# Turning a layer's softmax maxima in bfloat16, with buffers exchanged between queries, tokens and rows

## The chip, the cores and the metric

The kernel runs on one core of a Trainium2 chip. The metric is the device time of one execution in microseconds; the lower, the better. Before the change it is 1400.39 us (median of three runs, 1397.52 to 1403.52).

## What is computed

One transformer layer on x of shape (2, 2048, 256): layer norm, causal attention with 16 heads of 16, residual; layer norm, a gated feed-forward network whose inputs and weights are rounded to 4-bit floats in blocks of 16 (and scaled back), residual. Cut to what matters here:

```python
q, k = rope(split_heads(x @ Wq.T + bq)), rope(split_heads(x @ Wk.T + bk))
att = einsum('bhqd,bhkd->bhqk', q, k) / sqrt(16)
att = softmax(where(mask, att, -inf), axis=-1)
y = einsum('bhqk,bhkd->bhqd', att, v)
x = x + y @ Wo.T + bo
h = silu(fp4_linear(norm(x), w_gate)) * fp4_linear(norm(x), w_up)
x = x + fp4_linear(h, w_down)
```

## The kernel before, in words

Tokens are worked in chunks of 512 (`CH`; four chunks to a batch, eight in all), heads in four groups of four (`GROUP`). That gives 32 slots, one for each chunk and group. For a slot the kernel goes over the scores twice.

*Maxima* (`max_steps`, L1002). For each tile of 128 queries and each chunk of keys up to the diagonal, TensorE makes scores with queries on the partitions (L1020, two strips of 64 rows side by side, one for each of two heads; masks at L988 are bfloat16 matmuls added on the diagonal), and VectorE reduces them to row maxima (L1044). `split` (L1063 to 1085) puts each maximum into the tile `mslots` as a sum of three float32 numbers: of the first two only the upper 16 bits are kept, the third is what is left. `turn` (L1092) transposes `mslots` on TensorE, four times 128x128 (L1098, tile `ptm`), and ScalarE casts the result to the bfloat16 tile `mT` (L1104).

*Values* (`value_steps`, L1127). Scores are made again, this time with keys on the partitions: a bfloat16 matmul of `mT` with a matrix of -1 subtracts the maximum (L1150), a matmul of keys and queries adds the score (L1158), ScalarE takes the exponential (L1173), and TensorE multiplies with the values (L1206), with a column of ones for the denominator. `divide` transposes that back and divides.

The queries of a slot live in a tile `qT` (two head pairs x 512 tokens of float32, 4 KB on each partition), filled from a DRAM scratch `parts` by four DMAs (L866). A slot's maxima and its values both read it. The keys stay resident in `kT` (L879). Beside this run the side steps: the layer norm of the next chunk (tiles `xin`, read at L676, transposed at L694), its projections and rotary embedding (L763 to 879), the rounding of the weights (tile `wr`, which shares the room `xn` with the rows of the feed-forward network, L600), and the feed-forward network of chunks already attended (`ffn_steps`, L1316: rows `x0`, `x1`, `xn`, then L1430 gate and up, L1523 down, L1535 store). The last chunk's feed-forward network uses rooms that have come free, a `qT` room for each tile of 128 tokens.

The order of the work on each engine is not that of the code. Every step is a task with an engine, a cost and a due time, and names what it reads and writes. `Plan.ordered` (L158) plays the tasks through with those costs and picks, engine by engine, the one that can start first, or the most urgent of those that can start within 0.03 us of it. A task that makes a tile of some kind must find a room of that kind free: the dictionary `ROOM` says how many there are, the same number as the pool's buffers. So a count in `ROOM` or a task's cost changes the written order on all engines; the order is then fixed by dependencies between neighbouring instructions (`in_order`, L435). DMAs are all issued from one queue, SP's, in the planned order. A turn costs `turning(4)`, that is 0.01 + 0.13 x 4, in the plan.

Of the kernel before, what the change touches and what calls it, by code (L numbers as in the profile page):

```python
# [29 lines left out]
F32 = mybir.dt.float32  # L30
F32R = mybir.dt.float32r
BF16 = mybir.dt.bfloat16
# [6 lines left out]
P = 128  # L39
# [11 lines left out]
CH = 512  # L51
TPC = CH // P
# [29 lines left out]

XIN = 3
ROOM = dict(ps=7, av=1, ex=4, qT=5, parts=4)
ROOM.update(mx=2, mparts=1, left=1, mT=2, avs=1, den=2, y=2)
ROOM.update(xnT=1, xin=XIN, high=1, t1=1, t2=1, cs=1, dev=XIN-1)
ROOM.update(x0=1, xT=2, x1=2, xn=2, h=1, hrT=1, step=1, fdev=2, sc16=2, sc44=2)


ANY_TURN = ("ps",)
# [196 lines left out]
def turning(n):  # L289

    return 0.01 + 0.13 * n


def landing(kb):
    return 2.0 + kb / 250
# [3 lines left out]
def layer_kernel(  # L299
# [17 lines left out]
    nc = tc.nc  # L317
    B, T, E = x.shape
# [9 lines left out]


    const = ctx.enter_context(tc.tile_pool(name="const", bufs=1))  # L330
    qry = ctx.enter_context(tc.tile_pool(name="qry", bufs=5))
    spill = ctx.enter_context(
        tc.tile_pool(name="spill", bufs=4, space=bass.MemoryType.DRAM)
    )
# [3 lines left out]
    ffn = ctx.enter_context(tc.tile_pool(name="ffn", bufs=2))  # L338
    ps_s = ctx.enter_context(tc.tile_pool(name="ps_s", bufs=7, space=PSUM))
# [7 lines left out]
    ident = const.tile([P, P], F32, name="ident")  # L347
# [26 lines left out]
    for strip in range(2):  # L374
        rows = slice(strip * STRIP, (strip + 1) * STRIP)
# [11 lines left out]
        less.append(t)  # L387
    minus_half = const.tile([P, 1], F32, name="minus_half")
    nc.gpsimd.memset(minus_half, -0.5)
    mslots = const.tile([P, TPC, GROUP, SLOT], F32, name="mslots")  # L390
    nc.gpsimd.memset(mslots, 0.0)

# [35 lines left out]
    def small(cols, name):  # L428

        return ps_s.tile([P, CH], F32, tag="ps", name=name)[:, :cols]  # L430
# [160 lines left out]
    def load_rounded(w, row, rows, col, cols, put, target):  # L591

        st = {}
        raw = Thing("xn")
        scaled, rounded = fp4(lambda: st["raw"], raw, rows, cols)

        def load(due):
            def run():
                st["raw"] = ffn.tile([P, E], F32, tag="xn", name="wr", bufs=2)[:rows, :cols]
                nc.sync.dma_start(st["raw"], w[row : row + rows, col : col + cols])  # L600

            add(SP, landing(128), run, [], [raw], due)

        def turn(due):
            pm = Thing("ps")

            def run():
                pt = small(KE * P, "ptr").rearrange("p (k o) -> p k o", k=KE)
                for k in range(0, cols, P):
                    n = min(P, cols - k)  # L610
                    nc.tensor.transpose(
                        pt[:n, k // P, :rows], st["raw"][:, k : k + n], ident[:rows, :rows]
                    )
                st["pt"] = pt

            add(PE, turning(2), run, [raw, fixed], [pm], due, late=0.05)
            add(ACT, 0.35, lambda: put(st["pt"]), [pm], [target], due)

        return [(0, load), (3, scaled), (2, rounded), (4, turn)]
# [37 lines left out]
    def norm_steps(b, c):  # L657
# [5 lines left out]
        def load(i, due):  # L663
# [5 lines left out]
            def run():  # L669
                if not early:  # L670
                    st[i]["x"] = pre.tile([P, E], F32, tag="xn", name="xin", bufs=XIN)
                else:
# [329 lines left out]
    def max_steps(b, c, g):  # L1002

        steps = []
        st = {}
        mx, parts = Thing("mx"), Thing("mparts")
        found = []
        max_[b, c, g] = Thing("mT")

        def one(i, kc, d, due):  # L1010
            duo = 2 * (g % 2) + d
            cols = CH if kc < c else (i + 1) * P
            ps, got = (Thing("ps"), Thing("ps")), []

            def run():
                qT = qTs[b, c, g]
                kT = kTs[b, kc, g // 2]
                sc = [ps_s.tile([P, CH], F32, tag="ps", name="sc") for _ in range(2)]
                for h in range(2):
                    nc.tensor.matmul(  # L1020
                        sc[h][:, :cols],
                        lhsT=strips(qT, h, d, slice(i * P, (i + 1) * P)),
                        rhs=strips(kT, h, duo, slice(0, cols)),
                        start=True,
                        stop=(kc < c),
                    )
                if kc == c:
                    for h in range(2):
                        masked(sc, h, cols - P, mask_q)
                got.append(sc)  # L1030

            def reduced(h):
                name = "parts" if c else "mx"
                if name not in st:
                    st[name] = att.tile(
                        [P, TPC, 2, 2, NC] if c else [P, TPC, 2, 2],
                        F32,
                        tag=name,
                        name=name,
                        bufs=1 if c else 2,  # L1040
                    )
                at = st[name][:, i, h, d]
                dst = at[:, kc : kc + 1] if c else at.unsqueeze(1)
                nc.vector.tensor_reduce(dst, got[0][h][:, :cols], AX.X, ALU.max)  # L1044

            add(
                PE,
                0.18 + 0.44e-3 * cols if kc == c else 0.27,
                run,
                [qT_[b, c, g], k_[b, kc, g // 2][g % 2], fixed],  # L1050
                [*ps, m_order],
                due,
                [parts if c else mx],
                "strip",
                FEED_M,
                0.07,
            )
            for h in range(2):
                own = Thing(of=parts if c else mx)
                found.append(own)  # L1060
                add(DVE, on_vector(cols), lambda h=h: reduced(h), [ps[h]], [own], due)

        def split(due):  # L1063
            left = Thing("left")

            def run():
                if c:
                    st["mx"] = att.tile([P, TPC, 2, 2], F32, tag="mx", name="mx")
                    nc.vector.tensor_reduce(
                        st["mx"].rearrange("p i h d -> p (i h d)"),  # L1070
                        st["parts"][:, :, :, :, : c + 1].rearrange(
                            "p i h d k -> p (i h d) k"
                        ),
                        AX.X,
                        ALU.max,
                    )

                mx = st["mx"].rearrange("p i h d -> p i (h d)")
                rest = att.tile([P, TPC, GROUP], F32, tag="left", name="left", bufs=1)
                for n, (src, rest) in enumerate(((mx, rest), (rest, mslots[:, :, :, 2]))):  # L1080
                    part = mslots[:, :, :, n]
                    nc.vector.tensor_scalar(
                        part.bitcast(I32), src.bitcast(I32), UPPER, None, ALU.bitwise_and
                    )
                    nc.vector.tensor_tensor(rest, src, part, ALU.subtract)

            if c:
                add(DVE, 1.04, run, found, [mx, left, slots_of], due - 0.1)
            else:
                add(DVE, 0.79, run, found, [left, slots_of], due - 0.1)  # L1090

        def turn(due):  # L1092
            pm = Thing("ps")

            def run():
                st["pt"] = small(CH, "ptm").rearrange("p (i q) -> p i q", i=TPC)
                for i in range(TPC):
                    nc.tensor.transpose(  # L1098
                        st["pt"][:, i, :], mslots[:, i].rearrange("p s d -> p (s d)"), ident
                    )  # L1100

            def put():
                mT = att.tile([P, CH], BF16, tag="mT", name="mT")
                nc.scalar.copy(mT, st["pt"].rearrange("p i q -> p (i q)"))  # L1104
                maxima[b, c, g] = mT

            add(
                PE,
                turning(TPC),
                run,  # L1110
                [slots_of, fixed],
                [pm],
                due - 0.1,
                [max_[b, c, g]],
                late=0.05,
            )
            add(ACT, on_scalar(CH), put, [pm], [max_[b, c, g]], due - 0.1)

        for i in range(TPC):
            for kc in range(c + 1):  # L1120
                for d in range(2):
                    steps.append(lambda due, i=i, kc=kc, d=d: one(i, kc, d, due))
        return steps, split, turn

    rows, rows_ = {}, {}
# [563 lines left out]
    def transpose_biases(due):  # L1689
# [29 lines left out]
        lambda due, i=i, pair=pair: steps[0].stripped(i, pair, due)  # L1719
# [72 lines left out]
```

## Time and profile before

| | |
|---|---|
| Time, median of 3 runs | 1400.39 us (1397.52 to 1403.52) |
| The profiled execution's own time | 1400.22 us |
| Its span from the first to the last instruction | 1398.2 us |
| Mean granted TensorE clock | 0.976 |
| TensorE busy | 1338.2 us |
| VectorE busy | 1117.2 us |
| ScalarE busy | 759.6 us |
| GpSimd busy | 520.7 us |
| Moved by DMA | 69.22 MB, mean 50 GB/s |

All of these are of one profiled execution but the first row. PE is TensorE's matmuls, PEld its loads of weights, which overlap them; DVE is VectorE, ACT ScalarE, POOL GpSimd, SP the engine whose queue issues the DMAs. A group line names the code line, the engine, the operation, the tiles written and read, the shape and the count, then busy microseconds and mean nanoseconds of one, and last the idle time of the engine just ahead of these instructions with what ended it. A line of the time order has start, length (both in us), engine, line, operation and count. Matmuls are pipelined, so the length of one is more than its share of PE's time.

### The profile page before, as it was taken

To read this page: it belongs to the slowest core of one execution; us is meant where nothing else is said; L and a number is where in the kernel's file an instruction comes from. 1 tells how busy PE (TensorE), PEld (TensorE's weight loads), DVE (VectorE), ACT (ScalarE), POOL (GpSimd) and SP (SyncE) were. 2 spreads that over 40 slices of the span, in tenths; PEclk is the share of its full clock that TensorE was granted. 3 is DMA by queue.
4 is the path that set the end of the run, shared out by engine and by line. 5 is a ranking of instruction groups with operands and counts; after the bars stand their busy time and mean duration, and the time that the engine had idled before them with its cause. 6 is when DMAs were issued, how large, how long until landed. Compare 5 with 4: busy or idle time off the path is not lost. (4 is left out here: it accounts for less than half of the span.)

```text
span 1398.2 us, 27614 instructions
## 1 busy us (share of the span) xinstructions
PE 1338.2 (96%) x10437; PEld 675.2 (48%) x10437; DVE 1117.2 (80%) x2442; ACT 759.6 (54%) x1698; POOL 520.7 (37%) x671
## 2 busy tenths in 40 slices
PE   6898999999999999999999999999999999999986
PEld 3454445544544444444465455455454444444454
DVE  6779989988889988875477978998888988983286
ACT  2533665466556556567743455455655556667711
POOL 4655634434413433224353543242442331320342
PEclk9887999999999999999999999999999999999998
DMA  2443424202111301020422404130120120000000
GB/s 91 116 108 80 90 67 93 54 16 61 35 24 53 65 24 41 16 53 25 95 66 53 125 25 90 50 69 12 54 54 5 53 56 11 9 8 9 5 5 15
DMA packets 46316, 69.22 MB, mean 50 GB/s; under 512 B 6372, under 2 KB 22120, under 8 KB 46184
## 3 DMA queue, kind: packets, MB, share of 16 engines
q1 hardware_dynamic: 45888, 67.20, 20.4%
q8 instruction: 82, 1.34, 0.4%
q14 instruction: 50, 0.41, 0.1%
q10 hardware_dynamic: 296, 0.26, 0.1%
HBM read 47.52 MB, written 19.92 MB: 48 GB/s over the span
## 5 line engine op out<-in xcount | busy, mean ns | idle before, releaser
L1173 ACT ACTIVATE ex<-sx 128x512 f32<-128x512 f32 (+3 forms) x1280 | 594.0, 538 | 358.4 <-PE sx L1158 201.5
L1044 DVE TENSOR_REDUCE parts<-sc 128x1 f32<-128x512 f32 (+3 forms) x1152 | 638.9, 612 | 64.0 <-PE sc L1020 41.2
L1158 PE MATMUL sx<-qT,kT 64*128 64x512 f32 (+3 forms) x1280 | 339.2, 521 | 0.0
L1206 PE MATMUL av<-ex,v 128*32 128x512 f32 (+3 forms) x2560 | 300.6, 540 | 0.2 <-ACT ex L1173 0.2
L1020 PE MATMUL sc<-kT,qT 64*128 64x512 f32 (+3 forms) x1280 | 291.2, 430 | 9.1 <-DVE parts L1044 1.9
L1150 PE MATMUL sx<-mT,less 64*128 64x512 bf16 (+3 forms) x1280 | 249.5, 355 | 4.7 <-DVE mx L1044 2.0
L1020 PEld LDWEIGHTS sc<-kT,qT 64*128 64x128 f32 x1280 | 138.5, 190 | 156.9 <-DVE parts L1044 46.8
L517 POOL TENSOR_SCALAR inv<-inv 128x16 f32<-128x16 f32 (+2 forms) x82 | 18.0, 220 | 509.7 <-DVE inv L513 472.0
L1150 PEld LDWEIGHTS <-less 64*128 64x128 bf16 x1280 | 68.6, 94 | 211.1 <-issue 203.5
L1158 PEld LDWEIGHTS sx<-qT,kT 64*128 64x128 f32 x1280 | 132.6, 195 | 8.9 <-issue 6.5
L1523 PE MATMUL pd<-wdT,hrT 128*128 128x256 f32 (+1 forms) x384 | 103.6, 410 | 0.7 <-ACT hrT L1300 0.3
L1206 PEld LDWEIGHTS av<-ex,v 128*32 128x32 f32 x2560 | 52.0, 108 | 74.2 <-issue 65.9
L1523 PEld LDWEIGHTS pd<-wdT,hrT 128*128 128x128 f32 (+1 forms) x384 | 70.0, 197 | 29.8 <-issue 15.6
L1430 PE MATMUL pg<-wgT,xT 128*128 128x352 f32 x224 | 77.1, 478 | 1.0 <-ACT qb L776 0.3
L1044 DVE TENSOR_REDUCE mx<-sc 128x1 f32<-128x128 f32 (+3 forms) x128 | 54.6, 479 | 25.8 <-PE sc L988 25.6
L1430 PE MATMUL pg<-wuT,xT 128*128 128x352 f32 x224 | 74.3, 472 | 0.2
L763 PE MATMUL pj<-xnT,wqkT 128*128 128x512 f32 x128 | 73.3, 671 | 1.1 <-DVE v L954 0.6
L542 POOL TENSOR_TENSOR h<-h,step 128x704 f32<-128x704 f32 x28 | 47.2, 1686 | 68.6 <-DVE step L539 66.9
L988 PE MATMUL sc<-pick,mask_q 64*128 64x64 bf16 x1024 | 70.9, 201 | 0.0
L1456 ACT ACTIVATE h<-pg 128x352 f32<-128x352 f32 x64 | 30.0, 469 | 69.2 <-PE pg L1430 59.6
L815 POOL TENSOR_TENSOR t<-t,cs 128x512 f32<-128x512 f32 x31 | 39.6, 1279 | 75.1 <-DVE t L809 70.5
L988 PE MATMUL sx<-pick,mask_k 64*128 64x64 bf16 x1024 | 64.1, 196 | 0.0
(153 smaller groups left out, 1592.1 us busy)
## 6 DMA issues: line engine op xcount, KB each, us to landing
qT<-parts SPq DMA_DIRECT2D x120, 128.0 KB
kT<-parts SPq DMA_DIRECT2D x120, 128.0 KB
parts<-high SPq DMA_DIRECT2D x30, 256.0 KB
parts<-t SPq DMA_DIRECT2D x30, 256.0 KB
cs<-in_rope_dram SPq DMA_DIRECT2D x8, 512.0 KB
xin<-in_L_attn_x_dram SPq DMA_DIRECT2D x28, 128.0 KB
x<-in_L_attn_x_dram SPq DMA_DIRECT2D x28, 128.0 KB
out_dram<-x SPq DMA_DIRECT2D x28, 128.0 KB
```

What stands on the lines that cost most here:

```text
L542: queue.tensor_tensor(src(), src(), st["step"], ALU.add)
L763: nc.tensor.matmul(got["pj"], lhsT=wqkT[:, k, i, cols], rhs=xnTs[b, c][:, k, :], start=(k == 0), stop=(k == KE - 1),)
L815: (nc.gpsimd if early and i == 0 else queue).tensor_tensor(swapped, swapped, angles[b, c][:, 1, :], ALU.mult)
L988: nc.tensor.matmul(sc[h][:, col + at : col + at + STRIP], lhsT=strips(mask, h, half), rhs=strips(pick, h), start=False, stop=(half == 1),)
L1020: nc.tensor.matmul(sc[h][:, :cols], lhsT=strips(qT, h, d, slice(i * P, (i + 1) * P)), rhs=strips(kT, h, duo, slice(0, cols)), start=True, ...
L1044: nc.vector.tensor_reduce(dst, got[0][h][:, :cols], AX.X, ALU.max)
L1150: nc.tensor.matmul(sc[h][:, off:], lhsT=strips(less[d], h), rhs=strips(mT, h, slice(off, CH)), start=True, stop=False,)
L1158: nc.tensor.matmul(sc[h][:, off:], lhsT=strips(kT, h, duo, slice(jj, jj + P)), rhs=strips(qT, h, d, slice(off, CH)), start=False, stop=(j ...
L1173: nc.scalar.activation(st[j, d][:, h, off:], got[0][h][:, off:], AF.Exp, scale=HD**-0.5)
L1206: nc.tensor.matmul(st["av"][SLOT * s : SLOT * (s + 1), off:], lhsT=v[:, at : at + SLOT], rhs=st[j, d][:, h, off:], start=(j == 0), stop=(j ...
L1430: nc.tensor.matmul(got[half], lhsT=split("xrT")[:, k, :], rhs=wT[:, k, half * IH : (half + 1) * IH], start=(k == 0), stop=(k == KE - 1),)
L1523: nc.tensor.matmul(st["pd"], lhsT=st["hrT"][:n, k, :], rhs=wdT[:n, k, :], start=(k == 0), stop=(k == KI - 1),)
```

## The change

The maxima's transposes read the upper halves of the float32 numbers in `mslots` as bfloat16 (a view with a step of two), with an identity matrix in bfloat16, and write a bfloat16 tile in PSUM; ScalarE copies that to `mT`. Of the first two parts nothing is lost by that, since their lower halves are zero; the third part is cut to its upper half where before it was rounded. The turn's cost in the plan becomes 0.01 + 0.08 x 4. One VectorE cast makes the identity at the start. The rooms change: input tiles `xin` from 3 to 4 (and the small statistics tiles beside them, `dev`, from 2 to 3), row tiles `xn` from 2 to 3, query tiles `qT` from 5 to 4.

```diff
-XIN = 3
-ROOM = dict(ps=7, av=1, ex=4, qT=5, parts=4)
+XIN = 4
+ROOM = dict(ps=7, av=1, ex=4, qT=4, parts=4)
...
-ROOM.update(x0=1, xT=2, x1=2, xn=2, h=1, hrT=1, step=1, fdev=2, sc16=2, sc44=2)
+ROOM.update(x0=1, xT=2, x1=2, xn=3, h=1, hrT=1, step=1, fdev=2, sc16=2, sc44=2)
...
-    qry = ctx.enter_context(tc.tile_pool(name="qry", bufs=5))
+    qry = ctx.enter_context(tc.tile_pool(name="qry", bufs=4))
...
+    ident_b = const.tile([P, P], BF16, name="ident_b")
+    nc.vector.tensor_copy(ident_b, ident)
...
-                st["raw"] = ffn.tile([P, E], F32, tag="xn", name="wr", bufs=2)[:rows, :cols]
+                st["raw"] = ffn.tile([P, E], F32, tag="xn", name="wr", bufs=ROOM["xn"])[:rows, :cols]
...
-                st["pt"] = small(CH, "ptm").rearrange("p (i q) -> p i q", i=TPC)
+
+                upper = mslots.bitcast(BF16).rearrange("p i s (d two) -> p i (s d) two", two=2)
+                bank = ps_s.tile([P, TPC, P], BF16, tag="ps", name="ptm")
+                st["pt"] = bank
                 for i in range(TPC):
-                    nc.tensor.transpose(
-                        st["pt"][:, i, :], mslots[:, i].rearrange("p s d -> p (s d)"), ident
-                    )
+                    nc.tensor.transpose(st["pt"][:, i, :], upper[:, i, :, 1], ident_b)
...
-                turning(TPC),
+                0.01 + 0.08 * TPC,
```

## The prediction

> **What bounds the kernel now.** I read the page's busy row first, then the stages, then the groups of instructions, and last the instructions around one turn of the maxima.
>
> ```profile
> PE 1338.2 (96%) x10437; PEld 675.2 (48%) x10437; DVE 1117.2 (80%) x2442; ACT 759.6 (54%) x1698; POOL 520.7 (37%) x671
> ...
> PEclk9887999999999999999999999999999999999998
> ```
>
> TensorE leads, but a busy PE is not PE at its peak, so I ask where it is dense. Busy time by stage (columns: stretch, its length, then PE, PEld, DVE, ACT, POOL, the granted clock, DMA share, GB/s):
>
> ```profile
> 30.00:100.00 70.00, 63.06 (x524) 34.80 (x520) 53.73 (x149) 28.95 (x71) 40.80 (x60) 0.79 0.43 101
> 100.00:600.00 500.00, 487.99 (x3853) 239.14 (x3850) 438.07 (x954) 281.43 (x630) 196.12 (x249) 0.98 0.23 53
> ...
> 680.00:760.00 80.00, 77.06 (x716) 45.36 (x708) 49.67 (x128) 38.61 (x100) 30.09 (x37) 0.98 0.37 80
> 760.00:1270.00 510.00, 502.40 (x3984) 249.49 (x3982) 444.05 (x935) 292.54 (x639) 180.66 (x211) 1.00 0.18 43
> ...
> 1325.00:1398.20 73.20, 56.89 (x206) 38.23 (x206) 53.62 (x104) 11.83 (x35) 24.86 (x38) 0.88 0.03 11
> ```
>
> From 100 to 1325 us PE is 98 to 99% busy and DVE below 90%: there a microsecond of PE work taken out is nearly a microsecond of time. Before 100 us and after 1325 us PE waits for others. The last stage does not matter here: in the two instruction orders everything after the last value matmul on PE is the same.
>
> The step that the change touches is the turn of the maxima, by form and then by its row in the list of waits:
>
> ```profile
> L1098 PE MATMUL ptm<-ident,mslots 128*128 128x128 f32 x128 | 22.0, 298 | 8.4 <-DVE mslots L1085 3.3 <-DVE x L1390 2.5 <-DVE mx L1044 1.6
> ...
> L1104 ACT CAST mT<-ptm 128x512 bf16<-128x512 f32 x32 | 19.0, 592 | 36.4 <-PE ptm L1098 36.1
> ...
> L1098 PEld LDWEIGHTS ptm<-ident,mslots 128*128 128x128 f32 x128 | 14.6, 148 | 14.7 <-issue 5.8 <-DVE x L1390 2.6 <-DVE parts L1044 1.9
> ```
>
> Mean durations overlap, so they overstate the price. What PE pays is the distance from one start to the next. One turn in time order, with its neighbours:
>
> ```profile
> 704.90 0.47 PEld L1098 LDWEIGHTS ptm<-ident,mslots 128*128 128x128 f32 x4
> ...
> 705.01 0.60 PE L1098 MATMUL ptm<-ident,mslots 128*128 128x128 f32 x4
> ...
> 705.54 0.39 PE L1020 MATMUL sc<-kT,qT 64*128 64x256 f32 x2
> ...
> 705.76 0.12 PEld L988 LDWEIGHTS <-mask_q 64*128 64x128 bf16 x4
> 705.77 0.23 PE L988 MATMUL sc<-pick,mask_q 64*128 64x64 bf16 x4
> ...
> 705.84 0.37 PE L1020 MATMUL sc<-kT,qT 64*128 64x256 f32 x2
> ```
>
> Four matmuls of 0.273 us each fit in 0.60, so their starts lie (0.60 - 0.273)/3 = 0.109 us apart; the last is followed by the next strip matmul after 0.20. That is 0.53 us a turn here, and 32 turns. Summed over the trace, the 128 starts stand 19.9 us in all before what follows them, waits included. This is all that can be won at the turn.
>
> **The change part by part, bfloat16 turn.** It takes away 128 float32 transposes and adds 128 bfloat16 ones of the same 128x128 shape. No such row is in the trace. The nearest is the mask, bfloat16 with 128 weight columns and 64 moving ones: four of them, two on each half of the array, go by in 705.84 - 705.77 = 0.07 us, 0.035 us each on a half, loads of 128 columns included. Twice the moving columns is at most 0.07 us, and about 0.06 if part of the 0.035 does not grow with columns. Upper bound: no faster than float32, 0.109.
>
> Here the Trainium skill is weighed. "TensorE: Matmul & The Clock Gate", Part 4 (PE-mode transpose), gives a bfloat16 128x128 transpose in one kernel's context about 275 ns, which is the float32 row's 273 ns: by that rule the change wins nothing. The same page, Back-to-back issue gap, gives 81 ns for a load and matmul pair at 128 columns in a real kernel: an estimate of 4 x 32 x 0.028 = 3.6 us. Part 4's number is a latency, and the float32 row shows that a latency of 273 goes with a spacing of 109, so it does not decide. The mask row does, since it contains its loads: I take 0.06. The gain is 128 x (0.109 - 0.06) = 6.3 us (5.0 at 0.07, 3.6 by the page's gap, 0 at the upper bound). 28 of the 32 turns lie between 130 and 1300 us where PE is dense, and the few early ones at half clock cost double, so I let 90% through: -5.7 us.
>
> The first load of a turn also gets shorter (141 ns in float32 against 94 to 99 of the bfloat16 loads). It is exposed where the turn follows strip work, else it runs under the matmul before; half of 32 x 0.047 is -0.8 us (0 to -1.5). ACT's cast reads 512 columns either way, 0.592 us; I cost it at nothing, covered by ACT's 54%. What it waits for (36.1 us for the turn, 17 times) is idle time of an engine that is not the bound. DVE still writes all three parts of the maxima, so nothing goes there. The third part is now cut to bfloat16 and not rounded; that takes no time.
>
> **Identity in bfloat16.** One DVE cast of 128x128. The like cast of `less` took 0.23 us free and 2.10 us beside Pool's fills at 6 us. It stands on DVE after the two `less` casts, ahead of `fold` and of the first tile's statistics, which start at 8.90 us the moment DVE is free, and the first transposes of x at 10.96 wait for them: +0.5 us (0.2 to 2.1).
>
> **Rooms.** A fourth input tile, a third row tile and one query tile fewer move no work by themselves: the counts of all other instructions are equal. They change the planner's order. Up to the end the two PE orders keep step: at each turn from the eighth on, the counts of maxima, score and value matmuls done agree to within 12, mostly exactly. Within that PE changes between strip, value and whole-array work 1,144 times against 1,150. A change costs some 0.1 us (the turn above: 0.20 against 0.109 to the next matmul): -0.6 us.
>
> Does a query tile come too late with four? A tile may be refilled after the last score of the group four before. By counting instructions in the trace, that moment lies ahead of the group's first maximum by 33.6 us at the least (group 19: 687.2 and 720.9) and by 44 to 106 us in the others. So PE never waits for queries, if SP is free. But SP is one queue: an issue that waits holds all behind it. In the new order the second query tile of a pair slides behind input loads, stores or key loads. Only one place is tight: group 19's four query loads now stand inside the key loads for group 18.
>
> ```profile
> 686.62 5.11 SPq L879 DMA_DIRECT2D kT<-parts  x8
> ```
>
> Those ended at 691.7; the first use is at 699.7. A landing takes about 4.1 to 4.5 us (`parts<-high` 4.07, `x` 4.53 in the chain that ended last), so 3.7 us are to spare. Four more issues take 1.8 us and the tile is free at 687.2: still 1.9 us to spare, 0 us. If it failed, PE would pay each microsecond over that.
>
> **Sum** against the profiled execution's 1400.2 us (span 1398.2 and 2.0 around it; the median of the runs is 1400.39, the same): -5.7 - 0.8 - 0.6 + 0.5 = -6.6, so 1393.6 us.
>
> **Rivals.** *No gain* (0.20): bfloat16 transposes pass no faster, or DVE, 88% busy beside PE, takes the saved time as waits (the list of waits has 46.8 us of strip loads waiting for DVE's maxima): 1400.2 - 0.6 + 0.5, about 1400. For it: the page's 275 ns. Against: the mask rows.
>
> *More than the turn* (0.20): the extra tiles let side work into the first 142 us. There the granted clock is 0.5 in four stretches, one of them:
>
> ```profile
> 124.80:141.90 17.10, 14.05 (x64) 8.00 (x62) 16.69 (x45) 3.87 (x8) 7.59 (x12) 0.50 0.11 29
> ```
>
> DVE sets the pace in it (16.69 of 17.10) while PE starves. If half of one such stretch goes, about 4 to 5 us more: 1389.
>
> *Slower* (0.10): the same stretches grow. In the new order the maxima of group 2 end in 18 score matmuls in a row, of group 4 in 16, where before projections and weight turns stood between them. If PE is so sparse there that two more stretches of the length of the last, 17 us, run at half clock with PE's work on the path, each takes 17/2 = 8.5 us: 1393.6 + 17 = about 1410. It decides from the point where the loss passes the gain and the 7 us that can be told, 13.6 us: some 27 us at half clock beyond today's. Against: groups 2 and 4 are already at half clock today.
>
> **Numbers.** The likeliest case (0.50) is 1393.6, itself 1390 to 1398 by the bounds of 0.06 and of the share let through. About 0.5%, 7 us, is what a measurement can tell from no change: the line is at 1393.4. Of the likeliest case 0.2 falls under it; with *more* that is 0.40 faster; 0.50 the same; 0.10 slower. The range, 1387 to 1402, takes in *no gain* and most of *more*.
>
> **What would show it.** Matmuls of the turn about 0.06 us apart (right), or still 0.1 (the no-gain case). PE's busy time between 100 and 1325 us lower by about 5 us and its share unchanged; a share that falls means DVE took it. First x transposes at 11 to 11.5 us. Key loads of group 18 landed before its first maximum. Stretches at half clock in the first 142 us of about 48 us in all: a difference of 10 us there would make the prediction wrong either way.

## The result and the profile after

The changed kernel takes 1403.36 us (median of 17 runs, 1399.98 to 1408.32), the kernel before beside it on the same chip 1399.49 (17 runs, 1397.04 to 1403.52). The ratio is 1.0033, 95% interval 1.0023 to 1.0043: slower by about 4 us, where I had forecast 6.6 us faster. The profiled execution of the changed kernel took 1408.32 us, the slowest of its runs, so its trace shows more loss (8 us) than the median.

The page's busy row and the row of the granted clock, after:

```profile
PE 1341.4 (95%) x10437; PEld 673.4 (48%) x10437; DVE 1121.5 (80%) x2443; ACT 758.7 (54%) x1698; POOL 519.4 (37%) x671
...
PEclk9896899999999999999999999999999999999997
```

TensorE's busy time did not fall by the turn's 5 us; over the whole span it rose by 3, and from 100 to 1325 us it fell by 3 (1200.6 to 1197.5). The same stages as before, after the change (stretch, length, then PE, PEld, DVE, ACT, POOL, the granted clock, DMA share, GB/s):

```profile
30.00:100.00 70.00, 61.93 (x544) 34.63 (x540) 56.48 (x154) 29.57 (x75) 42.72 (x65) 0.83 0.42 106
100.00:600.00 500.00, 485.91 (x3801) 237.23 (x3802) 438.63 (x944) 278.89 (x622) 192.15 (x244) 0.97 0.23 54
680.00:760.00 80.00, 76.70 (x742) 44.22 (x740) 46.53 (x119) 41.93 (x107) 31.65 (x35) 0.96 0.39 87
760.00:1270.00 510.00, 501.51 (x3952) 247.44 (x3950) 440.95 (x939) 288.10 (x633) 182.21 (x213) 0.99 0.18 42
```

The share is nearly unchanged in each, but less work fits into each: 3,801 matmuls in the first long stage where 3,853 did before, 3,952 where 3,984 did. The clock is 0.01 lower in both. So the loss is spread over the dense middle; it is no single wait.

The turn itself did what I expected. Its instructions by tile (shortest/median/longest in ns, first and last start in us), then one turn in time order on PE:

```profile
L1103 PE MATMUL ptm<-ident_b,mslots x128: 216/219/314, 44.0 to 1281.5; 128*128 128x128 bf16 x128
```

```profile
709.22 0.39 PE L1103 MATMUL ptm<-ident_b,mslots 128*128 128x128 bf16 x4
```

Four matmuls of 0.219 us in 0.39 us: starts (0.39 - 0.219)/3 = 0.057 us apart. Over the trace the 128 starts now stand 14.1 us ahead of what follows them, where they stood 19.9: 5.8 us less. The same sums, from one PE start to the next, say where the profiled execution lost more than that: gate and up +3.9, value scores +3.8, maxima's scores +3.8, the subtraction of the maximum +2.4, projections +2.3, the transposes back +1.9, the transposes of x +1.6; against -4.4 for the masks of the value scores and -2.7 for the transposes of the feed-forward rows. No line stands out.

The clock did change. By the trace's clock records, the stretches at half clock sum to 68 us before and to 92 us after. Two of those of after lie in the middle; first the kernel after, then the kernel before over the same microseconds:

```profile
163.40:170.20 6.80, 6.80 (x53) 3.85 (x53) 4.46 (x16) 4.57 (x13) 4.15 (x9) 0.50 0.13 42
931.40:938.20 6.80, 6.76 (x25) 4.05 (x26) 5.51 (x11) 1.33 (x3) 1.97 (x3) 0.50 0.94 185
```

```profile
163.40:170.20 6.80, 5.94 (x62) 3.52 (x59) 5.53 (x16) 2.63 (x9) 2.79 (x5) 1.00 0.32 95
931.40:938.20 6.80, 6.70 (x43) 3.68 (x41) 6.60 (x20) 3.31 (x7) 2.23 (x6) 1.00 0.73 117
```

A stretch at half clock looks just as busy (6.76 of 6.80 us), with 25 matmuls in place of 43, though the two orders don't have the same work there. The clock differs from run to run of one kernel as well, and the time with it: pooled within the kernels of this study, a run whose mean clock is 0.001 lower is about 0.68 us longer (541 runs; the two go together, which of them drives the other is not shown). Since 0.001 is 2.8 us at half clock, a microsecond at half clock goes with about 0.24 us of time. The mean clock over all runs is 0.9755 before (236 runs) and 0.9712 after, which by that slope is 2.9 of the 4 us.

### The profile page after: what moved, and what is told of

Read it like the earlier page. It is cut to its first block, busy times and chain, and to the rows that moved or that the text cites. A ratio compares the mean times of both kernels' runs of the same rounds, so it can differ in the third digit from the quotient of the medians.

```text
span 1406.5 us, 27599 instructions
## 1 busy us (share of the span) xinstructions
PE 1341.4 (95%) x10437; PEld 673.4 (48%) x10437; DVE 1121.5 (80%) x2443; ACT 758.7 (54%) x1698; POOL 519.4 (37%) x671
## 4 chain that ended last, share of the span: by engine, by line
PE 68%; DVE 23%; POOL 4%; DMA 2%; issue 2%; ACT 1%; SPq 0%; POOLq 0%; DVEq 0%; ACTq 0%
PE av L1209 15%; PE pg L1433 10%; DVE parts L1046 10%; PE sc L1022 9%; PE sx L1153 9%; PE sx L1161 7%; PE pd L1526 5%; PE pj L765 4%; PE pth L1299 2%; PE po L1383 1%; DVE mx L1046 1%; PE pv L947 1%; DVE scale L511 1%; DVE step L538 1%; PE sx L990 1%
## 5 line engine op out<-in xcount | busy, mean ns | idle before, releaser
L1433 PE MATMUL pg<-wgT,xT 128*128 128x352 f32 x224 | 81.0, 495 | 2.1 <-DVE parts L1046 1.6
```

The lines of the kernel that those rows point to most:

```text
L1433: nc.tensor.matmul(got[half], lhsT=split("xrT")[:, k, :], rhs=wT[:, k, half * IH : (half + 1) * IH], start=(k == 0), stop=(k == KE - 1),)
```

## The experiments

The time of each kernel is its median, the ratio is to the kernel before, run beside it on the same chip (1398.85 to 1399.67 us). The clock is the mean over the kernel's runs; its standard error is 0.0004 to 0.0014. In the sums below the means of the times are used, against 1399.57 us for the kernel before (236 runs in five sets on four chips; the means of the sets differ by up to 0.5 us), with 95% intervals from the spread of the kernels' runs.

| Kernel | Time, us (runs) | Ratio (95%) | Clock |
|---|---|---|---|
| turn alone | 1401.20 (22) | 1.0015 (1.0006 to 1.0023) | 0.9717 |
| order alone | 1406.01 (5) | 1.0047 (1.0035 to 1.0059) | 0.9714 |
| turn and rooms | 1399.99 (14) | 1.0001 (0.9990 to 1.0012) | 0.9744 |
| turn and cost | 1403.23 (14) | 1.0024 (1.0012 to 1.0036) | 0.9714 |
| cost, float32 | 1407.03 (6) | 1.0049 (1.0033 to 1.0065) | 0.9702 |
| rooms, float32 | 1400.24 (22) | 1.0007 (1.0000 to 1.0014) | 0.9759 |
| cost 0.43, float32 | 1402.60 (22) | 1.0025 (1.0015 to 1.0035) | 0.9730 |
| cost 0.63, float32 | 1402.21 (22) | 1.0012 (1.0004 to 1.0021) | 0.9710 |
| fitting alone | 1401.08 (21) | 1.0012 (1.0003 to 1.0021) | 0.9741 |
| small tiles | 1399.45 (13) | 1.0001 (0.9992 to 1.0010) | 0.9751 |
| float32 turn twice | 1408.65 (6) | 1.0068 (1.0049 to 1.0087) | 0.9762 |
| a quarter of the divide's transposes | 1398.36 (22) | 0.9994 (0.9983 to 1.0005) | 0.9749 |
| VectorE more | 1406.26 (7) | 1.0056 (1.0037 to 1.0076) | 0.9749 |
| VectorE less | 1396.08 (22) | 0.9972 (0.9963 to 0.9981) | 0.9758 |
| VectorE less, and the turn | 1397.03 (22) | 0.9984 (0.9975 to 0.9993) | 0.9716 |
| ScalarE more | 1404.88 (12) | 1.0035 (1.0020 to 1.0049) | 0.9738 |
| turn by matmul | 1400.18 (14) | 1.0013 (0.9999 to 1.0027) | 0.9725 |
| bfloat16 turn twice | 1401.12 (22) | 1.0012 (1.0002 to 1.0022) | 0.9757 |

My theories changed on the way, and the expectations name some by a letter. First came A, the turn gains what was predicted and the order costs it back and more, against B, a lighter turn lets the clock fall and the order matters little. On where the gain went: P, PE alone sets the time, and a microsecond cut there is one gained; R, VectorE stands close behind and takes it back as waits; Q, neither of their loads but something else, say a latency. On the order: M, the planner was told of a cheaper turn and therefore does something particular; S, the order of before runs well, and any shift of it costs. On the clock: T, the gate counts transposes or their kind of instruction differently (K in one place); L, the stretch at a turn simply holds less work, and the gate lowers the clock.

### Turn and order apart

*Turn alone*: the bfloat16 turn in the order of before. To make room for the bfloat16 identity it takes the place of `pick` in the mask products, and two small tiles have one buffer; these are the "fitting" below.

```diff
-    pick = const.tile([P, STRIP], BF16, name="pick")
...
+    ident_b = const.tile([P, P], BF16, name="ident_b")
+    nc.vector.tensor_copy(ident_b, ident)
...
-                rhs=strips(pick, h),
+                rhs=strips(ident_b, h, slice(STRIP * h, STRIP * (h + 1))),
...
-                        st["pt"][:, i, :], mslots[:, i].rearrange("p s d -> p (s d)"), ident
...
+                    nc.tensor.transpose(st["pt"][:, i, :], upper[:, i, :, 1], ident_b)
```

> The bfloat16 turn in the instruction order of before: rooms 5, 3 and 2 and the old cost of the turn are kept; the bfloat16 identity takes the place of the mask's smaller one, and two small tiles that only VectorE uses have one buffer, so that it fits. Theory A (the turn is worth what was predicted, the new order of the instructions costs it back and more): 5 to 7 us faster than before, about 1393.5. Theory B (a lighter turn lets the granted clock fall more often, the order matters little): no faster than before, with clearly more than 68 us at half clock.

*Order alone*: the rooms and the plan's cost of after, and so its order, with the float32 turn.

```diff
-XIN = 3
-ROOM = dict(ps=7, av=1, ex=4, qT=5, parts=4)
+XIN = 4
+ROOM = dict(ps=7, av=1, ex=4, qT=4, parts=4)
...
-                turning(TPC),
+                0.01 + 0.08 * TPC,
```

> The order of after (its rooms and its planned cost) with the float32 turn. Theory A: slower than after by the turn's 5 to 6 us, so 9 to 10 us slower than before, about 1409. Theory B: about as before, 1399 to 1401, with about 68 us at half clock.

*Turn and rooms*: the bfloat16 turn and the new rooms, with the plan's old cost `turning(TPC)`.

> As after, but the plan keeps the old cost of the turn (0.53 in place of 0.33 us). Theory A, if the rooms make the order bad: as after, 1402 to 1405. Theory A, if the new cost makes it bad: near the turn alone, 1393 to 1396.

*Turn and cost*: the bfloat16 turn, fitted as in turn alone, and the new cost, with the old rooms.

> The turn alone, but with the plan's new cost of the turn: the rooms of before. Theory A, if the rooms make the order bad: near the turn alone, 1393 to 1396. If the new cost makes it bad: as after, 1402 to 1405. If each shift of the order moves the time by some microseconds, both this and the run with new rooms and old cost land in between.

The order alone costs 6.4 us (1406.00 against 1399.57 in the means), and the turn in that order gives 2.2 ± 1.2 of it back. That is the result of the change: +6.4 - 2.2. The 6.4 is well clear of noise. The 2.2 is less sure than it looks: the five runs of order alone lie within 0.4 us of each other, and with the spread that the other kernels have (2.3 us) the interval is about ± 2.4. The turn alone gains nothing, so A fails on the turn and B on the order. The new rooms with the turn are level with the kernel before; the new cost is not.

The same two hunks were run next with the float32 turn, each by itself.

```diff
-                turning(TPC),
+                0.01 + 0.08 * TPC,
```

> The float32 turn and the rooms of before; only the plan believes that a turn costs 0.33 us. So only the order of the instructions differs from before. If the order alone costs (any shift away from the order of before): 2 to 6 us slower. If it is the new rooms that make the order bad: as before, within 1.5 us.

```diff
-XIN = 3
-ROOM = dict(ps=7, av=1, ex=4, qT=5, parts=4)
+XIN = 4
+ROOM = dict(ps=7, av=1, ex=4, qT=4, parts=4)
...
-    qry = ctx.enter_context(tc.tile_pool(name="qry", bufs=5))
+    qry = ctx.enter_context(tc.tile_pool(name="qry", bufs=4))
```

> The float32 turn and the old cost in the plan, with the new rooms (four input tiles, three row tiles, four query tiles). If the rooms make the order bad: 4 to 7 us slower, like the order of after with the float32 turn. If any shift of the order costs: 2 to 6 us slower, and the other too.

A number in the plan, 0.33 where there was 0.53, costs 6.7 us with no instruction changed; the rooms cost 0.9. Is it that the plan believes in a cheaper turn? Two more kernels believe in 0.43 and in 0.63:

```diff
-                turning(TPC),
+                0.01 + 0.105 * TPC,
```

> The kernel before, float32 turn, old rooms; only the plan believes 0.43 us for a turn in place of 0.53. Theory S (the order of before is one that happens to run well, and any shift away from it costs): 2 to 6 us slower. Theory M (a plan that believes in a cheaper turn than the chip's is what costs): 2 to 4 us slower here, half of what 0.33 cost.

> The same with 0.63 us believed, so the order shifts the other way. Theory S: 2 to 6 us slower. Theory M: as before or faster, -3 to +1 us.

Both are slower, by 3.2 and 1.9 us in the means, one on each side of 0.53. In the measured time, then, M fails: it is not the direction of the belief. S comes near: the order of before is a good one, and four shifts away from it by the cost alone or with rooms (0.33, 0.43, 0.63, after's own) cost 2 to 7 us, while the shift by rooms alone costs about 1. Part of that goes with the clock (0.970 to 0.973 in these four, 0.9759 with the rooms alone). At equal clock, by the 0.68 us for 0.001, the order of after still costs 3.6 us; the belief of 0.33 costs 3.1 us, that of 0.43 costs 1.6, and that of 0.63 gains 1.2. In these three the rest does follow the belief, as M has it. So M is out for the time as a whole, not for the part that doesn't go with the clock; three kernels and a slope taken over from runs within a kernel don't decide it. The amount that is moved doesn't order the costs either: against before, PE has another kind of matmul in about 780 of some 10,200 places for 0.43, 1,740 for the rooms alone, 2,110 for 0.63 and 3,140 for 0.33. Which neighbourhoods in the order do it was not found.

Because turn alone contains the fitting, that was run without the turn, and its two small tiles without the mask's operand:

> The kernel before with the float32 turn and only what made room for the bfloat16 identity in the turn-alone runs: that identity in the place of the mask's smaller one, and one buffer for two small tiles that only VectorE uses. If these cost nothing: as before, within 0.5 us, and the 1.6 us of the run with the bfloat16 turn done twice stays unexplained. If they are that cost: 1.5 to 2 us slower at a clock of 0.975 to 0.976, and each turn-alone run has to be read against this one.

> The kernel before with only the one buffer for the two small tiles. If the waits that this adds on VectorE are the cost: as the run with room alone. If it is the identity: as before.

The fitting costs 1.6 us, about 1.0 of it with its clock, and little of it comes from the small tiles (0.3 ± 0.9); why the wider identity in the mask products costs this was not followed. So turn alone is to be read against the fitting alone: +0.2 ± 1.4 us (+0.6 when each is set against the kernel before on its own chip). On PE the turn is 7.6 us shorter there by the start-to-start sums (12.3 against 19.9 in the two traces), and it gains nothing in the order of before.

### Where the turn's microseconds go

First, does PE's work count at all? One kernel does the float32 turn twice: 14.0 us more at 0.109 us each, 14.8 by PE's start-to-start sums. One leaves out three of four transposes of the divide: 10.5 us less at 0.109 each, 7.0 by the sums, since after the one that stays the next matmul starts later (0.19 us in the median, 0.11 before).

```diff
-                for i in range(TPC):
+                for i in (*range(TPC), *range(TPC)):
```

> The kernel before, in its own order, with every float32 transpose of the maxima done twice, the second over the first: 4 x 0.109 us more of TensorE in each of 32 turns, 14.0 us in all. Theory P (TensorE alone sets the pace between 100 and 1325 us, as predicted): 11 to 14 us slower, about 1412. Theory R (TensorE, VectorE and ScalarE take turns through the seven PSUM banks, and a TensorE change at the turn is mostly met by waits): 2 to 6 us slower. If transposes count as activity for the clock, the granted clock is not lower than 0.976; if they don't, it is.

```diff
-                for i in range(TPC):
+                for i in range(1):
...
-                st["pt"] = pt
+                st["pt"] = pt[:, :1].to_broadcast([P, TPC, GROUP, SLOT])
```

> The kernel before, in its own order, with three of the four float32 transposes ahead of the division left out (the rows of the first tile stand for all four, so the attention's output is not the reference's): 3 x 0.109 us less of TensorE in each of 32 slots, 10.5 us in all. Theory P: 9 to 10 us faster, about 1390. Theory R: 1 to 4 us faster. If thinner TensorE work makes the granted clock fall, the clock is under 0.974 and the time as before or above.

Added work costs 8.6 of 14.8 us in the means, between what P (11 to 14) and R (2 to 6) had said. Work cut gives back 1.1 ± 1.1 of 7.0. PE is the bound on one side only: P falls. The busy rows of the two pages, first of the kernel with a quarter of the divide's transposes, then of the one with the float32 turn twice:

```profile
PE 1332.0 (95%) x10341; PEld 667.3 (48%) x10341; DVE 1117.5 (80%) x2442; ACT 759.9 (54%) x1698; POOL 520.7 (37%) x671
```

```profile
PE 1348.7 (96%) x10565; PEld 687.8 (49%) x10565; DVE 1119.3 (80%) x2442; ACT 760.5 (54%) x1698; POOL 520.4 (37%) x671
```

With 96 of its matmuls taken out PE still reads 95%. The share I had built on does not move with the work: it cannot tell a PE that is behind from one that is ahead and held up.

If VectorE holds it up, work added there costs and work cut there pays, and with VectorE relieved the turn should pay too. These kernels do the divide's multiplication twice (+13.6 us of VectorE, count times length), leave out the multiplication by the up product in one of the two halves of the hidden columns (-16.7 us), and leave it out with the fitted bfloat16 turn:

```diff
+                nc.vector.tensor_tensor(
...
+                    ALU.mult,
+                )
```

> The kernel before, in its own order, with VectorE's division of each slot done twice with the same result: 0.425 us more of VectorE in each of 32 slots, 13.6 us in all, none for TensorE. Theory P: 0 to 2 us slower. Theory R: 5 to 10 us slower.

```diff
+                if half:
+                    return
```

> The kernel before, in its own order, without the up product of the second half of the hidden columns (so the second half of the feed-forward network is not gated by it): 32 VectorE operations of 0.521 us less, 16.7 us in all. Theory R (VectorE and ScalarE, which empty the seven PSUM banks, set the pace that TensorE falls back to): 4 to 10 us faster. Theory Q (something that neither TensorE's turn nor VectorE's load moves, say a latency, sets the pace): no more than 2 us faster.

> The same with the bfloat16 turn, again in the order of before and with the same work left out. Theory R: with VectorE relieved the turn's TensorE time counts, so 3 to 5 us faster than the run with VectorE relieved alone, at the same granted clock. Theory Q: as that run, within 1 us, or slower by a lower clock.

And ScalarE, the copy of the values' sums made twice (+18.8 us):

```diff
+                nc.scalar.copy(st["avs"], st["av"])
```

> The kernel before, in its own order, with ScalarE's copy of the attended values done twice: 0.588 us more of ScalarE in each of 32 slots, 18.8 us in all. If ScalarE's emptying of PSUM banks is on the path that TensorE falls back to: 6 to 12 us slower, as more TensorE or VectorE work was. If it is not: 0 to 2 us slower.

In the means: VectorE more +6.8 of 13.6, VectorE less -3.5 of 16.7, ScalarE more +5.1 of 18.8. Each of the three engines costs when it gets more; of the two that were also relieved, TensorE and VectorE, each gives little. Of the 3.5 us some 1.3 lie at the end: 4 of the 32 multiplications left out stand behind the last value matmul, where TensorE is not dense, and from there to the end it is 72.6 us in this trace and 73.9 before. R is right that VectorE counts, and wrong that it alone holds the turn's gain: it had said 4 to 10 us from the relief and 3 to 5 more with the turn, and with VectorE relieved the turn makes +1.1 ± 1.3, not less. Q allowed at most 2 us from the relief; what is left for the dense part is near that, so Q is not ruled out. One rival is open: a piece done twice also lengthens a chain of steps that wait for each other (ScalarE's second copy holds the only `av` tile for 0.59 us more), and no run tells an engine's load from that delay.

The trace shows how a gain at one turn is lost. PE's loads of weights in time order around one turn, first before, then turn alone (the brackets: idle time ahead, and what ended it; "issue" is nothing that the profile shows):

```profile
364.20 0.42 PEld L1098 LDWEIGHTS ptm<-ident,mslots 128*128 128x128 f32 x4 [0.41 <-issue]
364.79 0.16 PEld L1206 LDWEIGHTS av<-ex,v 128*32 128x32 f32 x8 [0.17 <-issue]
365.14 0.30 PEld L1020 LDWEIGHTS sc<-kT,qT 64*128 64x128 f32 x4 [0.20 <-issue]
...
365.84 0.19 PEld L1158 LDWEIGHTS sx<-qT,kT 64*128 64x128 f32 x2
```

```profile
364.68 0.23 PEld L1099 LDWEIGHTS <-mslots 128*128 128x128 bf16 x4 [0.41 <-issue]
365.01 0.16 PEld L1206 LDWEIGHTS av<-ex,v 128*32 128x32 f32 x8
365.37 0.55 PEld L1018 LDWEIGHTS sc<-kT,qT 64*128 64x128 f32 x4 [0.20 <-issue]
...
366.33 0.19 PEld L1158 LDWEIGHTS sx<-qT,kT 64*128 64x128 f32 x2 [0.24 <-issue]
```

Count from the start of the turn. The values follow after 0.59 us before and after 0.33 in bfloat16: 0.26 us won. The value scores follow after 1.64 before and after 1.65: all of it is lost again within 1.7 us. It goes at the loads of the maxima's scores, whose group is 0.55 us long in place of 0.30. VectorE at the same time reduces three tiles of scores, first before, then turn alone:

```profile
364.51 1.88 DVE L1044 TENSOR_REDUCE parts<-sc 128x1 f32<-128x512 f32 x3
```

```profile
365.00 1.88 DVE L1042 TENSOR_REDUCE parts<-sc 128x1 f32<-128x512 f32 x3
```

It starts 0.31 us after the turn's start before and 0.32 in turn alone, so it has not moved with PE, and the first of the three reductions ends 0.99 us after the turn's start in both. In turn alone the trace names the end of that reduction (365.68 us) as what releases the second pair of score matmuls, at 365.70; before, it ended at 365.19, ahead of the second pair of loads at 365.25. The end of the next reduction then releases the second matmul of the subtraction in both kernels, 1.64 us after the turn's start before and 1.65 in turn alone. At this turn, then, VectorE takes the gain back: PE comes earlier and waits for a tile in PSUM that VectorE is still reading.

Where PE's starts of turn alone, and of the kernel with a quarter of the divide's transposes, are set beside those of before, most turns and divides end alike: PE gets ahead by about 0.26 or 0.33 us, and after 21 of the 32 turns and 25 of the 32 divides it is back within 0.06 us of the old distance within 7 us. The traces say what released PE just before it fell back: at the 21 turns VectorE 12 times, ScalarE 4 times, GpSimd once, and nothing that they show 4 times; at the 25 divides ScalarE 11 times, VectorE 9, GpSimd twice, nothing 3 times. With VectorE relieved it is still VectorE at 10 or 11 of 20 turns. So the engines that read PE's results set the pace at these places, and PE comes back to theirs. What is not shown is that more buffers would free the gain: a kernel with more room in PSUM would tell, but seven tiles for these scores and one for the values' sums are all that the kernel has, and it wasn't tried.

### Where the clock goes

The turn alone has a lower clock, 0.9717 against 0.9741 of the fitting alone, though its order is that of before. One kernel makes the bfloat16 turn by ordinary matmuls with the identity, in place of transposes, and one makes the bfloat16 transposes twice, so that a turn is about as long as in float32:

```diff
-                        st["pt"][:, i, :], mslots[:, i].rearrange("p s d -> p (s d)"), ident
+                    nc.tensor.matmul(
+                        st["pt"][:, i, :], lhsT=upper[:, i, :, 1], rhs=ident_b, start=True, stop=True
```

> The turn alone in the order of before, but as an ordinary bfloat16 matmul with the identity into float32, and not as a transpose: the same columns through TensorE. Theory T (a transpose in bfloat16 doesn't count as activity, and that is why the clock fell to 0.972): clock back at 0.975 to 0.976 and about 1397 us. Theory L (TensorE has less to do in the windows around a turn, whatever the instruction): clock about 0.972 and about 1401 us, as the turn alone.

```diff
-                for i in range(TPC):
+                for i in (*range(TPC), *range(TPC)):
```

> The bfloat16 turn in the order of before, each transpose done twice: 8 x 0.056 us, so TensorE is as long at the turn as with float32. Theory L (less TensorE work in the stretch around a turn is what lets the clock fall): clock back at 0.975 to 0.976, time as before, 1399 to 1400. Theory K (the kind of instruction lets it fall): clock 0.972, 1401 to 1403.

The matmuls give the same low clock as the transposes, 0.9725 (standard error 0.0008) against 0.9717 (0.0006), so T falls. Doubled, the transposes bring it back to 0.9757 (0.0005), and the time is the same to 0.1 us as with one set. That fits L: a shorter turn leaves less work in a stretch, and the clock falls there. It does not prove L. The kernel with a quarter of the divide's transposes has 7.0 us less on PE too, and its clock, 0.9749 (0.0007), is not clearly under that of before; and the orders of 0.33 and 0.63 come to 0.970 and 0.971 with the float32 turn.

Nor do single stretches show it. In the profiled execution of turn alone three stretches at half clock that before does not have lie at turns, from 60, 159 and 890 us. Two of the three the fitting alone has as well, with its float32 turn, from 61.8 and 157.3 us. The second of turn alone, and then the same turn on PE in turn alone, in the fitting alone and in before:

```profile
159.20:162.60 3.40, 3.10 (x16) 1.01 (x15) 1.79 (x7) 0.59 (x1) 1.56 (x4) 0.50 0.00 0
```

```profile
159.50 0.58 PE L1099 MATMUL ptm<-ident_b,mslots 128*128 128x128 bf16 x4 [2.35 <-DVE x L1390]
```

```profile
157.52 1.12 PE L1096 MATMUL ptm<-ident,mslots 128*128 128x128 f32 x4 [2.13 <-DVE x L1388]
```

```profile
160.04 0.66 PE L1098 MATMUL ptm<-ident,mslots 128*128 128x128 f32 x4 [2.48 <-DVE x L1390]
```

PE had idled 2.1 to 2.5 us ahead of this turn in all three. Turn alone and the fitting alone then ran it at half clock; before, with the longest idle time of the three, ran it at full clock (0.66 us for the four float32 transposes in place of 1.12). So this stretch falls with the float32 turn too, and each trace is one execution. Only the mean clocks carry the point; why the clock falls with the shorter turn stays open.

Put at equal clock by the slope of 0.68 us for 0.001, the turn gains in all five pairs of one order: 1.4 us (turn alone against the fitting), 1.5 (turn and rooms against rooms), 1.8 (with VectorE relieved), 2.3 (after against order alone), 3.3 (turn and cost against cost). The third and the fifth still contain the fitting. PE's starts stand 7.2 to 7.8 us closer in each of these pairs of traces. So a fifth to two fifths of that would come through the balance of the engines; in the orders with the clock of before, 1.0 to 2.9 us would then go with a lower clock, while in the orders of the new cost the clock is low already and nothing more goes. This is worked out and not measured: it takes the slope found within kernels to hold between them.

## Why the prediction was wrong, step by step

**Spacing of the transposes: right.** 0.06 us was taken from the mask row, 0.056 is the median in the trace. The mask row gave only an upper bound of 0.07, so the nearness of 0.06 is partly luck. The turn's 6.3 us measured 5.8 from before to after, with two orders in that, and 7.2 to 7.8 between kernels of one order. The loads were right as well: 98 ns in place of 141, where 94 to 99 was taken.

**"There a microsecond of PE work taken out is nearly a microsecond of time": the step that failed first.** I let 90% of the turn through, -5.7 us. It was 0 in the order of before and about 2.2 in that of after. PE's share from 100 to 1325 us was the reason (I read 98 to 99%; it is 98% over all, and 96% from 680 to 760 us in the row that I showed), and the quarter of the divide's transposes shows that it proves nothing for a cut: 7.0 us less on PE, 1.1 us gained. PE came sooner to work that VectorE or ScalarE had not yet released, as at the turn at 364 us, where VectorE's reductions took 0.26 us back. The *no gain* rival named VectorE for this, and I gave it 0.20; VectorE is the one most often, but not alone, and its relief didn't free the gain. The sign that I set for it did not work: in a stretch of fixed length, busy time and share are the same reading. And the list of waits does not show it. Strip loads waiting for VectorE's maxima (total us, times, longest us), in before, turn alone, order alone and after:

```profile
PEld sc L1020 <- DVE parts L1044: 46.8, 87, 0.8
```

```profile
PEld sc L1018 <- DVE parts L1042: 45.5, 84, 0.8
```

```profile
PEld sc L1020 <- DVE parts L1044: 52.8, 93, 1.5
```

```profile
PEld sc L1022 <- DVE parts L1046: 51.4, 89, 1.5
```

This wait grew with the order, by 6.0 us with the float32 turn, and not with the turn.

**Order: the step that turned the sign.** I counted it at -0.6 us, from 1,144 changes of tiling against 1,150. It was +6.4, and with the 2.2 at the turn that makes the 4 us lost. The two orders agreed in how far each was with maxima, scores and values at every turn, and I took this for the same pace. The plan's cost of the turn was the hunk that did it, one that I had not priced at all: it adds no instruction, but it moves many. What in the new order costs the time was not found. The counts gave no price for it; its bounds should have been several microseconds on either side.

**Clock: kind right, size and place wrong.** The *slower* rival (0.10) asked for more time at half clock and priced 27 us of it at half each. The mean clock says about 12 us more (0.0043 at 2.8 us for 0.001), which goes with 2.9 us. Each goes with 0.24 us and not 0.5; the reason was not tested. And it does not come in the first 142 us, where I looked: in the profiled execution the stretches there sum to 48 us in both kernels, as I had said. All of the growth lies later, 44 us in place of 20, with stretches from 163, 788 and 931 us on where before has none.

**The rest held.** VectorE in time order, after:

```profile
6.12 2.02 DVE L391 CAST ident_b<-ident 128x128 bf16<-128x128 f32 x1
...
9.21 0.42 DVE L472 BATCH_NORM_STATS2 stats<-first 128x6 f32<-128x256 f32 x1
```

The cast's 2.02 us are mostly waiting behind the `less` cast in front of it: the reduction that stood in its place before is 1.95 us long there and 0.35 in after. The first statistics start at 9.21 in place of 8.90 us, +0.3 where I took 0.5, and the first transposes of x at 11.28, in the range I gave. The rooms are near neutral (+0.9 in float32). With four query tiles SP's queue does wait for one, in 6 places and up to 21 us:

```profile
SPq L868 <- PE sx L990: 67.3, 6, 21.4
```

and no wait of PE for queries or keys followed, as I had said.

## What to carry to other kernels

TensorE, dense as it was, set the time for work that was added and not for work that was taken away. Where VectorE and ScalarE feed such an engine through few buffers, cut a few microseconds by an experiment (leave out a piece of about that size) before counting on them. A cost in a planner is a change of the program like any other: price a new order with bounds of several microseconds, and separate it from the edit by running each without the other. Compare the granted clock over all runs of each kernel, not over one profile, before a small difference is put down to an instruction.

## What the runs showed of the hardware

A 128x128 transpose in bfloat16 follows the one before after 0.056 us, in float32 after 0.109 (medians of after and of before), with lengths of 219 and 273 ns; as ordinary bfloat16 matmuls they have the same spacing and length, and the time is the same within the runs' spread (1400.5 ± 1.7 against 1401.4 ± 1.0 us).

The granted clock of this kernel, with TensorE 95% busy, moved with small changes: with the turn's few microseconds made shorter its mean went from 0.974 to 0.972, and with the short turn made twice it was 0.976. In one execution of each, the same turn, behind 2.1 to 2.5 us of idle time, ran at half clock in two kernels and at full clock in a third. The Trainium skill, "TensorE: Matmul & The Clock Gate", Part 4 (PE-mode transpose), says of a transpose that it doesn't count as busy for the gate in the same way. Here transposes and matmuls in their place leave the same clock, 0.9717 and 0.9725, so the runs do not show that difference.
